# The last chunk's transposes after layer 0's projection: a new order of left-over pieces at the start of the attention

## The chip, the cores and the metric

The kernel runs on one core of one Trainium2 chip. The metric is the device time of one execution in microseconds (us), as the median of several runs. The engines are TensorE (PE in the profile; PEld is its weight load), VectorE (DVE), ScalarE (ACT), GpSimd (POOL) and SyncE (SP), which issues most of the DMAs.

## The reference

Two layers work on an image `x` of 2 x 128 x 64 x 64 in float32. Layer 0 is a neighbourhood attention with an MLP behind it; layer 1 is a full attention over 4096 tokens per image, and then a spectral convolution. What matters here, cut:

```python
# layer 0, for each image, on x transposed to tokens
y = _ln(x, g1, be1)
y = _na2d(y, qkv_w, qkv_b, rpb, proj_w, proj_b)   # 7 x 7 neighbourhood, 4 heads, then proj
y = _ln(y, g2, be2) @ w1.T + bl1
x = y + r
y = relu(_ln(x, g3, be3) @ w2.T + bl2)
x = _ln(y, g4, be4) @ w3.T + bl3 + x
# layer 1
t = _to_tokens(x)
q = _ln_t(t)
sim = einsum('blh,bmh->blm', q, q) * scale          # diagonal masked
t = t + einsum('blm,bmh->blh', softmax(sim), q)
t = t + _L1_ffn_ref(_ln_t(t), ...)                   # spectral filters, as a convolution
```

## The kernel before, in words

**Layer 0** is cut into 16 bands, eight for each image, of 8 rows x 64 columns = 512 tokens. The work on one band is cut into some 70 small pieces, each a closure kept by name: `p.` for the projections to q, k and v, `u0` to `u3` for the four attention units, `r.` for the division by the softmax's sum, `t.`, `t1.`, `t2.`, `t3.` for the output projection and the MLP with its norms. A table, `PLAN`, gives each piece a time; a band is started each `PERIOD`. All pieces of all bands are sorted by these times into one list of events, which is executed with a manual schedule: the order written is the order on PE, DVE, ACT and POOL.

**Pieces of the next layer among them.** While image 1 goes through layer 0, image 0 is prepared for the attention of layer 1, in eight chunks of four token tiles, one chunk for each band of image 1. These pieces begin with `k.`: `k.a` (transposes of `xa`, L196), `k.tt` (copy by ScalarE, L683), `k.bn` (statistics by VectorE, L690 and L692), `k.pw` (the power -1/2 by POOL, L697 and L698), `k.z` (four normalised tiles `tok` by POOL, L703), `k.b` (four transposes of `tok` by TensorE, recorded at L189 with inputs `ident,tok`) and `k.cm` (the copy to `cm` by ScalarE, L715).

**What is left over.** Pieces of the last bands that would come after the last attention unit of layer 0 aren't executed there. They are put into the list `later` (65 pieces of the bands 12 to 15: the ends of the MLP and the norms); the seven `k.` pieces of the last band are put into `chunk_`. The list executed later is `chunk_` followed by `later`. The first pieces of `later` are `t.proj` of band 15 (the output projection, four products at L601, which read `att`), `t.pb` of band 15 (VectorE adds the bias, L612), `t.yr` of band 12 (POOL, L659), `t.add` of band 12 (POOL, L635 and L637) and `t3.bn` of band 12 (VectorE, L378 and L380). Behind them stand, among others, `t3.pw` (POOL, L385 and L386), `t3.nb` (VectorE, L395), `t3.zd` (VectorE, L415), `t3.za` (ScalarE, L406), the same five of `t1` for band 15, `t3.tr` (transposes of `z`, L189), `t3.zT` (copy by ScalarE, L428) and `t.w3` (the product at L332).

**The attention of layer 1** takes pairs of chunks (a, c), a <= c. For a pair, `weights` makes four products of 128 x 512 (L898), of which ScalarE makes the exponentials `e` with their sums (L905); where a = c VectorE adds the diagonal first (L903). For a = c the products with `tok` go onto `own` (L926). For a < c they go onto `other` (L951), and the exponentials are also turned: `turned` transposes four 128 x 128 blocks into a bank (L912), and VectorE copies them out as `et` and adds up their sums (L915); the products of `et` go onto `own` (L926). The products of the next pair are issued ahead of those of this one.

**What is filled in.** After each product the attention calls `fill`, which takes one step of the first generator that has one. The first is `drain`: it executes the left-over list, three pieces to a step. Here the order isn't manual: the framework's scheduler orders the instructions of the attention and of the pieces, by its own plan, on each engine. In it the last chunk's `k.b` of before stands on TensorE behind three of the first four products onto `own`, and ahead of the third product of the pair (0, 1) and of `t.proj`. The banks that the pieces and the attention use come from one ring of six.

**Other work at this place.** `branch_weights` (VectorE, L1068 to L1109; POOL raises `sg` to a power at L1065) and `filters` (VectorE copies `pn` to `ph`, L1142, from DMAs that SP issues at L1136) run through the same stretch. Behind the attention of image 0 comes that of image 1, and then the convolution (products at L1306, copies at L1307, products with the filter matrices at L1318).

Of the kernel before, what the change touches and what calls it, by code (L numbers as in the profile page):

```python
# [93 lines left out]
def kernel(  # L94
# [125 lines left out]
    with l0a:  # L220
# [611 lines left out]
        now, later, chunk_ = [], [], []  # L832
        for at, k, name, f in events:
# [4 lines left out]
            else:  # L838
                early = True
            (chunk_ if name[:1] == "k" and k == bands[-1] else now if early else later).append(f)  # L840
        later = [*chunk_, *later]
        engines = mybir.EngineType
        with tc.manual_schedule(engines={engines.PE, engines.DVE, engines.Activation, engines.Pool}):
            for f in now:
# [649 lines left out]
```

## Time and profile before

| what | value |
|---|---|
| runs | 2232.13, 2233.68, 2233.82 us; median 2233.68 |
| the profiled execution | 2235.26 us, of which the span from the first to the last instruction is 2233.6 us |
| mean granted TensorE clock over the span | 0.991 |
| layer 1's attention, first product of image 0 (L898) | starts at 352.6 us |
| layer 1's attention, last product of image 1 (L898) | starts at 1284.4 us |
| one product of 128 x 512 (L898, L926, L951) at full clock | 0.86 us in the chain |

The profile is of one execution. Its times count from the span's start. TensorE's float32 products of 128 x 512 stand in it as two records each; a transpose of 128 x 128 is one record. A matmul's own duration holds the time until its last result, so following ones overlap it; the chain of waits gives the pace. "Idle before" and the name behind the arrow say how long an engine stood ahead of an instruction, and what was finished last before it went on. The granted clock is the share of full speed that TensorE had in a stretch.

### The profile page before, as it was taken

The numbers are of one execution on the slowest core, as the hardware profiler recorded it, in microseconds if no ns is written. First come the engines' busy times: TensorE is split into PE (matmuls) and PEld (weight loads), VectorE is DVE, ScalarE is ACT, GpSimd is POOL, SyncE is SP. The second block draws the span as 40 slices with busy tenths as digits, with TensorE's granted clock in tenths as the row PEclk, the third lists the DMA queues.
The fourth block names the chain that finished last, engine by engine and source line by source line (L and its number), as shares of the span: only waits on it lengthen the run. The fifth ranks groups of instructions, "written<-read, shape, count | busy, mean of one in ns | idle before, by whom it ended". The sixth has DMA issues, their size and how long they took to land.

```text
span 2233.6 us, 31536 instructions
## 1 busy us (share of the span) xinstructions
PE 2165.4 (97%) x11856; PEld 1333.8 (60%) x11856; DVE 932.9 (42%) x3038; ACT 783.4 (35%) x1904; POOL 276.7 (12%) x353
## 2 busy tenths in 40 slices
PE   5899998999999999999999999999999999999998
PEld 3577774544454444544544447677677777777766
DVE  4799985434443346433333342222213232323232
ACT  2789983222332223222222332322323232222232
POOL 3367874200000000000000000000000000000000
PEclk8999998999999999999999999999999999999999
DMA  4222222011000016100000122222222121212101
GB/s 110 72 62 61 61 55 51 1 57 62 24 24 22 8 44 181 38 24 15 10 24 24 47 82 68 50 48 59 47 51 59 39 59 39 59 39 59 40 10 76
DMA packets 174810, 109.53 MB, mean 49 GB/s; under 512 B 26049, under 2 KB 159809, under 8 KB 174146
## 3 DMA queue, kind: packets, MB, share of 16 engines
q1 hardware_dynamic: 171818, 105.24, 18.0%
q10 hardware_dynamic: 2840, 2.27, 0.4%
q8 instruction: 94, 1.54, 0.3%
q14 instruction: 58, 0.48, 0.1%
HBM read 72.87 MB, written 34.60 MB: 48 GB/s over the span
## 4 chain that ended last, share of the span: by engine, by line
PE 86%; DVE 6%; POOL 3%; DMA 2%; ACT 1%; issue 1%; SPq 1%; ACTq 0%; POOLq 0%; DVEq 0%
PE acc L1318 25%; PE pc L1306 13%; PE bank L898 10%; PE own L926 10%; PE other L951 8%; PE bank L912 4%; PE bank L332 2%; PE bank L189 2%; PE bank L542 2%; PE bank L1011 1%; PE bank L1043 1%; PE py L1340 1%; DMA st<-in_m_minus_dram 1%; PE po L564 1%; PE bank L506 1%
## 5 line engine op out<-in xcount | busy, mean ns | idle before, releaser
L1307 DVE COPY y<-pc 128x512 f32<-128x512 f32 x320 | 221.6, 692 | 351.5 <-PE pc L1306 347.8
L905 ACT ACTIVATE e<-bank 128x512 f32<-128x512 f32 x288 | 171.9, 597 | 552.5 <-PE bank L898 417.3
L898 PE MATMUL bank<-cm 128*128 128x512 f32 x576 | 298.9, 603 | 1.4 <-DVE y L653 1.4
L1318 PE MATMUL acc<-y,mpl 128*128 128x256 f32 x1280 | 292.1, 382 | 0.0
L1318 PE MATMUL acc<-y,mmi 128*128 128x256 f32 x1280 | 288.0, 379 | 0.0
L1306 PE MATMUL pc<-ct,ut 64*128 64x512 f32 x1280 | 285.2, 595 | 0.9 <-issue 0.9
L1318 PEld LDWEIGHTS acc<-y,mpl 128*128 128x128 f32 x1280 | 238.1, 190 | 59.4 <-issue 29.6
L1318 PEld LDWEIGHTS acc<-y,mmi 128*128 128x128 f32 x1280 | 242.6, 190 | 32.7
L1307 ACT COPY y<-pc 128x512 f32<-128x512 f32 x320 | 205.0, 641 | 86.5 <-PE pc L1306 86.5
L951 PE MATMUL other<-e,tok 128*128 128x512 f32 x448 | 228.6, 592 | 0.0
L926 PE MATMUL own<-et,tok 128*128 128x512 f32 x448 | 227.1, 594 | 1.4 <-DVE part L915 1.4
L915 DVE CUSTOM_DVE_ANT_0 et<-bank,one 128x512 f32<-128x512 f32 x224 | 145.7, 688 | 166.5 <-PE bank L912 166.3
L1306 PEld LDWEIGHTS pc<-ct,ut 64*128 64x128 f32 x1280 | 121.5, 187 | 145.8 <-issue 140.6
L1325 ACT COPY ob<-acc 128x256 f32<-128x256 f32 x32 | 19.3, 604 | 387.0 <-PE acc L1318 387.0
L926 PEld LDWEIGHTS own<-et,tok 128*128 128x128 f32 x448 | 84.4, 190 | 109.7 <-issue 72.6
L951 PEld LDWEIGHTS other<-e,tok 128*128 128x128 f32 x448 | 85.0, 190 | 106.6 <-issue 105.9
L898 PEld LDWEIGHTS bank<-cm 128*128 128x128 f32 x576 | 95.7, 193 | 73.8 <-issue 44.7
L1342 DVE TENSOR_TENSOR xa<-py,xa 128x512 f32<-128x512 f32 x32 | 22.1, 692 | 281.4 <-PE py L1340 281.4
L912 PEld LDWEIGHTS bank<-ident,e 128*128 128x128 f32 x896 | 103.3, 142 | 57.2 <-issue 43.6
L161 POOL TENSOR_TENSOR ln_rs<-ln_rs,mhalf 128x4 f32<-128x4 f32 x24 | 24.3, 1012 | 847.6 <-DVE ln_rs L160 847.6
L529 ACT ACTIVATE p<-p,mn 128x196 f32<-128x196 f32 x256 | 114.4, 449 | 22.2 <-DVE mn L519 14.0
L912 PE MATMUL bank<-ident,e 128*128 128x128 f32 x896 | 117.6, 274 | 0.0
(208 smaller groups left out, 2292.4 us busy)
## 6 DMA issues: line engine op xcount, KB each, us to landing
ut<-us SPq DMA_DIRECT2D x80, 256.0 KB
us<-ub SPq DMA_DIRECT2D x64, 256.0 KB
vw<-vd SPq DMA_DIRECT2D x256, 49.0 KB
ct<-gs SPq DMA_DIRECT2D x160, 72.0 KB
ct<-gs SPq DMA_DIRECT2D x160, 64.0 KB
gs<-sum SPq DMA_DIRECT2D x20, 256.0 KB
vd<-v SPq DMA_DIRECT2D x128, 32.0 KB
st<-in_m_plus_dram SPq DMA_DIRECT2D x16, 256.0 KB
```

The lines of the kernel that those rows point to most:

```text
L189: nc.tensor.transpose(ps[:, j * P : (j + 1) * P], src[:, j, :], ident)
L332: nc.tensor.matmul(pl, lhsT=wg[:, lo : lo + P], rhs=zT, start=True, stop=True)
L529: nc.scalar.activation(p, p, AF.Exp, bias=t[name + "mn"][:, h : h + 1], scale=-1.0, accum_out=t["den"][:, u, h : h + 1],)
L898: nc.tensor.matmul(ps, lhsT=cm[b][:, n * P : (n + 1) * P], rhs=cm[b][:, chunk(c)], start=True, stop=True)
L905: nc.scalar.activation(e, ps, AF.Exp, bias=0.0, scale=ASCALE, accum_out=part[:, n, c : c + 1])
L912: nc.tensor.transpose(pt[:, k * P : (k + 1) * P], es[k][:, m * P : (m + 1) * P], ident)
L915: nc.vector.tensor_tensor_reduce(et, pt, one, 1.0, 0.0, ALU.mult, ALU.add, part[:, n, a : a + 1])
L926: nc.tensor.matmul(own, lhsT=tok[b][:, n, :], rhs=e, start=first, stop=last)
L951: nc.tensor.matmul(other, lhsT=tok[b][:, 4 * CHUNKS[a] + j, :], rhs=es[j], start=(j == 0), stop=(j == 3))
L1306: nc.tensor.matmul(pc, lhsT=ut[fp, b, par, :], rhs=cv_[fp], start=True, stop=True)
L1307: (nc.scalar.copy if f else nc.vector.tensor_copy)(y[:, 4 * f : 4 * f + 4, :, par, b * 2 * FB + q : (b + 1) * 2 * FB : 2], pc.rearrange("p ...
L1318: nc.tensor.matmul(acc, lhsT=(mmi if l else mpl)[:, k, :], rhs=y[:, 1::2, k, ::-1, :] if l else y[:, 0::2, k, :, :], start=(l == 0 and k = ...
```

## The change

The list of left-over pieces is no longer `chunk_` and then `later`. In the diff, `chunk_[:3]` is `k.a`, `k.tt`, `k.bn`; `later[2]` is `t.yr` of band 12; `chunk_[3:5]` is `k.pw`, `k.z`; `later[:2]` is `t.proj`, `t.pb` of band 15; `later[3:5]` is `t.add`, `t3.bn` of band 12; `chunk_[5:]` is `k.b`, `k.cm`. So `t.yr` comes ahead of `k.pw`, and the four other pieces of `later` come ahead of the chunk's transposes. From the thirteenth piece on the list is the same.

```diff
@@ -838,7 +838,8 @@
             else:
                 early = True
             (chunk_ if name[:1] == "k" and k == bands[-1] else now if early else later).append(f)
-        later = [*chunk_, *later]
+
+        later = [*chunk_[:3], later[2], *chunk_[3:5], *later[:2], *later[3:5], *chunk_[5:], *later[5:]]
         engines = mybir.EngineType
         with tc.manual_schedule(engines={engines.PE, engines.DVE, engines.Activation, engines.Pool}):
             for f in now:
```

The pieces are the same ones and compute the same. On the built program's instruction lists, those of POOL, VectorE and SP have the order of before. On TensorE the order after the second product onto `own` is now: third product of the pair (0, 1), third product onto `own`, the four of `t.proj`, fourth product of the pair, fourth onto `own`, the four transposes of `k.b`. Before it was: third product onto `own`, the four transposes of `k.b`, third product of the pair, the four of `t.proj`, fourth product of the pair, fourth onto `own`. On ScalarE, `k.cm` now stands behind the exponentials of the third and fourth product of the pair and behind `t3.za`, and both halves of `t1.za` stand ahead of the exponentials of the pair (0, 2). Four of these allocations (`k.b`, `t.proj`, third and fourth product of the pair) get another bank of the ring.

## The prediction

> **What bounds the kernel now.** I read the page's shares first, then the chain of waits, then the timelines of the engines around the change. From the page:
>
> ```profile
> PE 2165.4 (97%) x11856; PEld 1333.8 (60%) x11856; DVE 932.9 (42%) x3038; ACT 783.4 (35%) x1904; POOL 276.7 (12%) x353
> ...
> PE 86%; DVE 6%; POOL 3%; DMA 2%; ACT 1%; issue 1%; SPq 1%; ACTq 0%; POOLq 0%; DVEq 0%
> ```
>
> TensorE is the bound nearly everywhere, so a time lost on it is a time lost at the end, unless another queue then becomes late. A part of POOL's 3% of the chain lies just where the attention begins. The chain there (start, us, what):
>
> ```profile
> 356.32 1.76 POOL y L659
> 358.09 3.29 POOL sg L1065
> ...
> 362.82 3.37 POOL tok L703 x4
> ...
> 366.24 0.48 PE bank L189
> 366.71 1.71 PE bank L898 x2
> 368.42 1.71 PE bank L601 x8
> 370.13 1.69 PE bank L898 x2
> 371.81 0.86 PE own L926 x2
> ```
>
> POOL ends last until 366.2: its queue is unbroken, and its last four instructions (k.z) make the tokens that the last chunk's transposes (k.b, L189) read. Then TensorE takes over, and each job of it costs 1.7 us where the same job costs 0.86 us from 371.8 on. TensorE's timeline says what it did meanwhile (the brackets are the idle time ahead):
>
> ```profile
> 359.10 1.88 PE L926 MATMUL own<-e,tok 128*128 128x512 f32 x4
> 363.68 0.33 PE L189 MATMUL bank<-ident,tok 128*128 128x128 f32 x1 [2.70 <-POOL tok L703]
> 364.68 0.37 PE L189 MATMUL bank<-ident,tok 128*128 128x128 f32 x1 [0.68 <-POOL tok L703]
> 365.46 0.47 PE L189 MATMUL bank<-ident,tok 128*128 128x128 f32 x1 [0.41 <-POOL tok L703]
> 366.24 0.48 PE L189 MATMUL bank<-ident,tok 128*128 128x128 f32 x1 [0.30 <-POOL tok L703]
> ```
>
> TensorE stands for 2.70 + 0.68 + 0.41 + 0.30 = 4.09 us, with ready products queued behind the waiting transposes. The busy times by stretch (columns: PE, PEld, DVE, ACT, POOL, granted clock, DMA) show the second half of the price:
>
> ```profile
> 361.00:362.00 1.00, 0.00 (x0) 0.00 (x0) 1.00 (x9) 0.00 (x0) 0.92 (x3) 1.00 1.31 113
> 364.00:365.00 1.00, 0.32 (x2) 0.14 (x1) 0.48 (x2) 0.00 (x0) 1.00 (x2) 0.92 1.28 69
> 371.00:372.00 1.00, 1.00 (x2) 0.33 (x2) 1.00 (x8) 0.15 (x1) 0.00 (x0) 0.67 0.05 15
> ```
>
> Between the last two rows the clock is 0.50. A mean of 0.92 puts the fall at 364.84, one of 0.67 the return at 371.66. The idle stretch thus costs twice: the wait, and a slow start after it.
>
> [...]371.66 - 364.84 = 6.82 us, two windows. [...]VectorE's L1142 pair runs at 368.14, behind an L395 that waited 3.06 us for POOL.
>
> **The change part by part.** Steps moved: t.yr and t.add of band 12 (1 and 3 POOL instructions), t3.bn of band 12 (8 on VectorE), t.proj and t.pb of band 15 (4 products; 1 on VectorE), k.pw and k.z (2 and 4 on POOL), k.b (4 transposes) and k.cm (1 on ScalarE). None issues a DMA. In the built program the orders on POOL, VectorE and SP are those of before (the scheduler had them there already); only TensorE and ScalarE change. So POOL still ends k.z at 366.2, and those three orders cost nothing.
>
> TensorE: four jobs now stand ahead of the transposes: an L898, t.proj's L601 (eight records), an L898 and an L926, each 0.86 us at full clock: 3.44 us. The PE queue would end them at 360.85 + 3.44 = 364.3. The transposes then go as tokens come, the last at 366.24, and the next L898 starts at about 366.36. The four jobs' inputs are all early: att was written at 348.7, the exponentials that free their banks ended by 358.6.
>
> Without a new wait the first L926 on a turned tile (378.54 in before) is reached after L898, L951, L898, L951, L912 x8, L898, L951: 7 x 0.86 = 6.0, at 372.4. In before the same road from 366.36 has eleven jobs: 11 x 0.86 = 9.5, which gives 375.85 at full clock; the trace has 378.54, so 2.7 us went to half clock (5.42 us of work between 366.24 and 371.66, half of it lost: 2.71).
>
> The clock in after: the idle time left is about 1.5 us, scattered over 364.3 to 366.2. A window holding all of it is still 56% busy. Windows of before that I could lay on the grid: 14% busy lost the clock, 60 to 80% mostly kept it (the one from 334.11, 60% and made of small products, lost it). I take full clock; the other end is one or two half-clock windows, 1.7 to 3.4 us of TensorE time.
>
> New wait, VectorE: the turned tile needs L915, which stands behind the statistics of band 15. VectorE in before:
>
> ```profile
> 368.14 0.67 DVE L1142 COPY ph<-pn 128x256 f32<-128x256 f32 x2
> 370.17 0.69 DVE L612 TENSOR_TENSOR x<-bank,add 128x512 f32<-128x512 f32 x1 [1.36 <-PE bank L601]
> ...
> 373.52 0.16 DVE L395 SCALAR_TENSOR_TENSOR ln_nb<-ln_mv,ln_rs 128x4 f32<-128x4 f32 x1 [1.48 <-POOL ln_rs L386]
> 373.60 0.60 DVE L415 TENSOR_SCALAR z<-x,ln_mv,ln_rs 128x128 f32<-128x128 f32 x2
> ```
>
> L612 no longer waits for L601 and follows L1142 at 368.75, 1.42 us sooner. Its chain keeps its lengths: statistics, POOL's power, L395 3.35 us after L612, both L415 done at +3.96, so L915 can start at 372.7 and its tile is there at 372.7 + 0.70 = 373.4; with the semaphore 373.5. TensorE, there at 372.4, waits **1.1 us**. Behind that L926 stand four transposes of z and all later products. So the start moves from 378.54 to 373.5: **5.0 us** in this execution. L915 of before started at 376.58 only because TensorE was late; the cover is now gone, and each us that VectorE is later costs one.
>
> ScalarE: both halves of t1.za (L406) now stand ahead of the exponentials of the next pair. L395 then ends at 372.26, so L406 takes 372.3 to 373.2 and the first such exponential 373.1 to 373.7; the product that wants its bank (the L898 after L926 and the transposes) comes at 374.8. The exponential that L912's fourth transpose reads stays behind t3.za, which POOL's power holds until 367.7: it runs 368.5 to 369.2; TensorE asks at 369.8. Covered by 0.6 us. L912's second tile now uses t.proj's bank, freed by L612 at 369.4, wanted at 370.2. All cost nothing; each turns into a wait if its margin goes. k.cm ends at about 369.8 and only the transposes of z, at 374.4, ask for its bank.
>
> After that the order is that of before, and TensorE ends last again, so 5.0 us should reach the end: 2235.26 (the profiled execution, 2233.6 of span and 1.7 around it) becomes 2230.2.
>
> Against the median of the runs: the grid lies differently in each. [...]work at half clock after 366.24 lasts 3.4 to 6.8 us and costs 1.7 to 3.4[...]. I take 2.4, an estimate, not this execution's 2.7. Then 375.85 + 2.4 - 373.5 = 4.7 us, and 2233.68 - 4.7 = **2229.0**. The 373.5 hangs on POOL and VectorE and does not vary with the grid; the spread is 3.5 to 5.9 us, 2227.8 to 2230.2.
>
> **The rivals.** *The clock falls all the same*, as the remaining 1.5 us may fall into one window[...]. For: the 60% window from 334.11. Against: windows from 351.18 and 852.94, about as empty, kept it. 1.7 to 3.4 us of loss, of which the 1.1 us of waiting at L926 hide part: the gain shrinks to 2.4 to 4.1, 2229.6 to 2231.3.
>
> *The wait moves on*: VectorE or ScalarE is one to three us later than worked out (L395's chain, or the 0.6 us margin at L912), TensorE stands for 2 to 4 us at L926: 2229.9 to 2231.9. For: three margins below 1 us. Against: each length is read from rows of these very instructions.
>
> *No second wait*: L926 at 372.4, a gain of 4.7 + 1.1 = 5.8 us, or 6.8 if the longest half-clock stretch is typical: 2226.9 to 2227.9.
>
> *Slower*: VectorE's second L1142 pair waits for a transfer of phi; it stands ahead of L612 and so of L915. In before it was hidden by up to 5 us, now by nothing: one us per us beyond 368.1. Its gain is gone when it lands 4.7 us late, and it is over 0.2% slower from 9.2 us late, 10 us giving 2239.0. Against: the first pair's transfer ended its wait at 363.67, and the second was issued 1.4 us after it.
>
> That the change does nothing is excluded by the instruction order.
>
> **Chances.** As worked out 0.70, clock falls 0.11, wait moves on 0.10, no second wait 0.06, slower 0.03. 0.2%, about what a measurement of this kernel can tell from no change, is 4.5 us: below 2229.2 is faster. The likeliest case straddles that line, with a little more than half below (0.40 of 0.70), and no second wait lies wholly below it; the early ends of the two next cases add little, and the runs' own 1.7 us spread blurs it: faster 0.50, same 0.46, slower 0.04. The range, 2226.8 to 2232.3, takes in the rivals but the slower one, with 0.6 to 1 us for the spread of runs.
>
> **What would show it.** Right: L189 on tok begins near 364.3 with under 1 us of listed idle in all; L898 behind it 0.86 us, not 1.7; no clock of 0.5 between 364 and 372; L612 at about 368.8 without waiting; TensorE idle about 1 us ahead of the first L926 on et, released by VectorE L915, at about 373.5; the attention's end some 5 us sooner. Wrong: half clock after 366, an idle above 2 us at L926 or L912, a wait of L898 for ScalarE's e near 375, or later waits that take the gain back.

## The result, and the profile after

| what | before | after |
|---|---|---|
| median of 13 runs each, taken together | 2235.32 us (2232.13 to 2237.53) | 2231.14 us (2227.11 to 2233.32) |
| ratio, with its 95% interval | | 0.9979 [0.9970, 0.9987] |
| the profiled execution | 2235.26 us | 2231.67 us |
| its span | 2233.6 us | 2229.9 us |
| the attention's first product of image 0 | 352.57 us | 352.94 us |
| POOL ends `k.z` | 366.18 us | 366.19 us |
| first product of a turned tile onto `own` | 378.54 us | 373.42 us |

The ratio says 4.7 us faster (0.0021 x 2235), between 2.9 and 6.7; the single times of one kernel spread by more than that. The diff adds an empty line, so lines behind it count one more: L899 is L898 of before, L913 L912, L916 L915, L927 L926, L952 L951, L1066 L1065, L1143 L1142. The page's shares moved little:

```profile
PE 2162.2 (97%) x11856; PEld 1332.3 (60%) x11856; DVE 932.4 (42%) x3038; ACT 781.9 (35%) x1904; POOL 276.3 (12%) x353
...
PE 85%; DVE 6%; POOL 4%; DMA 2%; ACT 1%; SPq 1%; issue 1%; ACTq 0%; POOLq 0%; DVEq 0%
```

TensorE lost 3.2 us of busy time, with the same 11856 instructions; some 2.7 of them are the products that ran at half clock at this place in before. The chain of waits around the change (start, us, what):

```profile
362.80 3.39 POOL tok L703 x4
366.19 0.21 POOL ln_rs L385
...
368.82 0.61 DVE x L612
...
371.01 1.05 POOL ln_rs L386
...
372.76 0.60 DVE et L916
...
373.42 1.13 PE own L927 x2
```

In before the chain went from POOL's `tok` into TensorE's transposes. Now it never touches TensorE between 362.80 and 373.42: it stays with POOL, goes through VectorE's bias and statistics and POOL's second power, and comes to TensorE with `et`. TensorE's timeline shows both stretches, with the idle time in brackets:

```profile
363.79 1.02 PE L927 MATMUL own<-e,tok 128*128 128x512 f32 x2
364.65 0.38 PE L189 MATMUL bank<-ident,tok 128*128 128x128 f32 x2
365.47 0.33 PE L189 MATMUL bank<-ident,tok 128*128 128x128 f32 x1 [0.44 <-POOL tok L703]
366.25 0.33 PE L189 MATMUL bank<-ident,tok 128*128 128x128 f32 x1 [0.45 <-POOL tok L703]
366.41 1.02 PE L899 MATMUL bank<-cm 128*128 128x512 f32 x2
...
373.42 1.13 PE L927 MATMUL own<-et,tok 128*128 128x512 f32 x2 [0.82 <-DVE part L916]
```

Two transposes find their tile ready; two wait 0.89 us together, where four waited 4.09 us before. The product behind them is 0.86 us ahead of the next, not 1.7. And there is a wait that before did not have: 0.82 us for `et`. (From start to start it is 373.42 - 371.58 = 1.84 us for a job of 0.86, so 0.98 lost.) The busy times by stretch (PE, PEld, DVE, ACT, POOL, granted clock, DMA share, GB/s) have full clock at the place where before had half:

```profile
364.00:365.00 1.00, 1.00 (x4) 0.28 (x2) 0.70 (x2) 0.00 (x0) 1.00 (x2) 1.00 1.66 106
365.00:366.00 1.00, 0.36 (x2) 0.14 (x1) 0.00 (x0) 0.00 (x0) 1.00 (x2) 1.00 0.35 27
371.00:372.00 1.00, 1.00 (x3) 0.38 (x2) 0.00 (x0) 0.00 (x0) 0.99 (x1) 1.00 0.06 16
```

VectorE's timeline shows why `et` comes when it does:

```profile
368.73 0.69 DVE L612 TENSOR_TENSOR x<-bank,add 128x512 f32<-128x512 f32 x1
...
372.08 0.16 DVE L395 SCALAR_TENSOR_TENSOR ln_nb<-ln_mv,ln_rs 128x4 f32<-128x4 f32 x1 [1.48 <-POOL ln_rs L386]
372.16 0.60 DVE L415 TENSOR_SCALAR z<-x,ln_mv,ln_rs 128x128 f32<-128x128 f32 x2
372.67 0.68 DVE L916 CUSTOM_DVE_ANT_0 et<-bank,one 128x512 f32<-128x512 f32 x1
```

L612 no longer waits for L601. The tile's copy stands behind L395, which waits 1.48 us for POOL. It starts at 372.67 and takes 0.69 us, while TensorE has ended the job before (371.58 + 0.86 = 372.44) and has nothing else ahead of this product.

**The gain at the place.** From the end of `k.z` to the first product of a turned tile it was 12.35 us and is 7.23. It adds up: four jobs of 0.86 us are gone from this road (3.44), the half clock is gone (2.7: half of the 5.42 us between the last transpose at 366.24 and the clock's return at 371.66; what 12.35 leaves over 0.2 for the last transpose and 11 jobs x 0.86 is 2.7 too), and the new wait is added (0.98). 3.44 + 2.7 - 0.98 = 5.16, against 5.12 seen. Against a second profile of before (run e9 below, 11.13 us) the gain is 3.9, since the half clock took less there. The two mean 4.5, which fits the 4.7 of the timing.

The end of `k.z` is at 366.18 and 366.19 us by a coincidence: the attention began 0.37 us later in after, and POOL's power for `sg` took 2.93 us there against 3.31.

**Why the two profiles differ by less at the end.** The spans differ by 3.6 us. What lies between is the same to 0.1 us but for two stretches in which the clock fell in one of the two executions: at 859.8 us in before, of which 0.2 us is left over by 920 us, and at 1292.2 us, where the attention gives way to the convolution, in after. The latter in the busy times of after:

```profile
1292.00:1296.00 4.00, 4.00 (x12) 1.47 (x12) 0.87 (x2) 1.67 (x2) 0.00 (x0) 0.57 0.07 18
```

The clock is 0.57 there, and it is 1.00 in before. In both traces every half-clock stretch lasts 3.41, 6.83 or 20.48 us, that is one, two or six times 3.41, but for the last one, which the end of the trace cuts; "window" below means such a piece of 3.41 us. From the attention's last product onto `own` to the first product of the convolution it is 37.65 us in after and 35.95 in before. Such a fall begins between 1289 and 1296 us in three of the six profiles with the transposes early (e2, e3, e5) and in three of the six with the transposes late (after, e1, e8), so these 1.7 us at the end belong to the execution and not to the change: 5.1 + 0.2 - 1.7 = 3.6.

### The profile page after: what moved, and what is told of

Same layout as the page of the kernel before. It is cut to its first block, busy times and chain, and to the rows that moved or that the text cites. A ratio compares the mean times of both kernels' runs of the same rounds, so it can differ in the third digit from the quotient of the medians.

```text
span 2229.9 us, 31535 instructions
## 1 busy us (share of the span) xinstructions
PE 2162.2 (97%) x11856; PEld 1332.3 (60%) x11856; DVE 932.4 (42%) x3038; ACT 781.9 (35%) x1904; POOL 276.3 (12%) x353
## 4 chain that ended last, share of the span: by engine, by line
PE 85%; DVE 6%; POOL 4%; DMA 2%; ACT 1%; SPq 1%; issue 1%; ACTq 0%; POOLq 0%; DVEq 0%
PE acc L1319 25%; PE pc L1307 13%; PE own L927 10%; PE bank L899 9%; PE other L952 8%; PE bank L913 4%; PE bank L332 2%; PE bank L189 2%; PE bank L1044 2%; PE bank L542 1%; PE bank L1012 1%; PE py L1341 1%; DMA st<-in_m_minus_dram 1%; PE po L564 1%; PE bank L506 1%
## 5 line engine op out<-in xcount | busy, mean ns | idle before, releaser
L899 PE MATMUL bank<-cm 128*128 128x512 f32 x576 | 296.8, 599 | 1.4 <-DVE y L653 1.4
L927 PE MATMUL own<-et,tok 128*128 128x512 f32 x448 | 227.3, 594 | 3.4 <-DVE part L916 3.4
L952 PE MATMUL other<-e,tok 128*128 128x512 f32 x448 | 228.6, 592 | 0.0
L916 DVE CUSTOM_DVE_ANT_0 et<-bank,one 128x512 f32<-128x512 f32 x224 | 145.6, 688 | 164.6 <-PE bank L913 164.5
L927 PEld LDWEIGHTS own<-et,tok 128*128 128x128 f32 x448 | 84.2, 190 | 112.4 <-issue 71.1
L952 PEld LDWEIGHTS other<-e,tok 128*128 128x128 f32 x448 | 85.0, 190 | 106.6 <-issue 106.2
L899 PEld LDWEIGHTS bank<-cm 128*128 128x128 f32 x576 | 95.2, 192 | 73.8 <-issue 44.4
L913 PEld LDWEIGHTS bank<-ident,e 128*128 128x128 f32 x896 | 102.9, 141 | 56.5 <-issue 41.9
L913 PE MATMUL bank<-ident,e 128*128 128x128 f32 x896 | 117.2, 274 | 0.0
```

Of the source, the lines that this page charges most:

```text
L899: nc.tensor.matmul(ps, lhsT=cm[b][:, n * P : (n + 1) * P], rhs=cm[b][:, chunk(c)], start=True, stop=True)
L913: nc.tensor.transpose(pt[:, k * P : (k + 1) * P], es[k][:, m * P : (m + 1) * P], ident)
L916: nc.vector.tensor_tensor_reduce(et, pt, one, 1.0, 0.0, ALU.mult, ALU.add, part[:, n, a : a + 1])
L927: nc.tensor.matmul(own, lhsT=tok[b][:, n, :], rhs=e, start=first, stop=last)
L952: nc.tensor.matmul(other, lhsT=tok[b][:, 4 * CHUNKS[a] + j, :], rhs=es[j], start=(j == 0), stop=(j == 3))
```

## The experiments

The theory: three sizes make the gain, namely four jobs in the place of TensorE's idle time, a clock that no longer falls, less a new wait for VectorE. Rivals: the clock is no cost of its own; the cause is another order of POOL's and VectorE's pieces, or ScalarE's; the gain is POOL's, whose work ends last on the chain. ScalarE's new order and the other banks have no run of their own. But in before TensorE lists no wait for ScalarE or for a bank between 359 and 379 us, so there was none that they could have removed.

**1. The transposes later, alone.** The list without the other moves: `t.yr` stays behind `k.z`.

```diff
-        later = [*chunk_, *later]
+        later = [*chunk_[:5], *later[:4], later[4], *chunk_[5:], *later[5:]]
```

> The transposes of the last chunk stand behind t.proj and behind the two products around it, as in the changed kernel, but t.yr of band 12 keeps its place behind k.z in the list. The scheduler then also puts L612 ahead of the first L395 on VectorE. Theory (the gain is the four TensorE jobs that now fill POOL's stretch, and the clock that stays up): from the end of k.z on POOL to the first product of own on a turned tile about 7 us as in the changed kernel (7.2), not 12.4 as in before; idle time ahead of the transposes about 1 us; no half clock behind them; because L612 is early, the wait ahead of that product shrinks from 0.8 to about 0.5 us. Rival (moving t.yr ahead of k.pw is what helped): 10 us or more. One time, about 2231 us in the first case, near 2235 in the second.

Measured: 2232.97 us in one run, a time that occurs with both kernels and so decides nothing. From the end of `k.z` to the turned tile's product it is 6.85 us, the transposes wait 0.25 + 0.45 us, and the clock does not fall there. TensorE and VectorE at this place:

```profile
373.27 1.12 PE L926 MATMUL own<-et,tok 128*128 128x512 f32 x2 [0.44 <-DVE part L915]
```

```profile
362.68 0.66 DVE L612 TENSOR_TENSOR x<-bank,add 128x512 f32<-128x512 f32 x1
```

So the place of the transposes makes the gain at this spot, and the order of `t.yr` makes none of it. The order is not quite that of the change in this build: `t.proj` stands two products earlier on TensorE, and VectorE has L612 six microseconds sooner than after the change (362.68 against 368.73). TensorE's wait for `et` is 0.44 us, not 0.82, which is the 0.4 us by which this road is shorter than after the change.

**2. Kept busy while it waits.** Before's order, with five products ahead of the last chunk's transposes; the transposes overwrite their results. They take the idle time. The scheduler also moves one product onto `own` behind the transposes.

```diff
+            if b == NB - 1 and g == NG - 1:
+                for _ in range(5):
+                    nc.tensor.matmul(t["kb"], lhsT=cm[0][:, 0:P], rhs=cm[0][:, 0:512], start=True, stop=True)
```

> The order of before, with five additional products of 128 x 512 into the transposes' own bank ahead of them; the transposes overwrite them, so nothing is left out. TensorE still waits for POOL's last token tile, but is kept busy for 4.3 us of the wait. The scheduler moves one product of own behind the transposes (0.86 us). Theory (the wait cost twice, once as idle time and once as half clock): no half clock behind the transposes, and from the end of k.z to the first product on a turned tile 0.2 + 12 x 0.86 = 10.5 us instead of 12.4 in before's profile; time about 1.5 us below before (2.4 of half clock less 0.9 for the moved product). Rival (the half clock is no cost of its own, the idle time is all): 12.4 + 0.9 = 13.3 us, and 0.9 us above before. Second rival[...]: half clock from about 365 as in before.

Measured: median 2235.87 us of 13 runs, beside 2234.98 of 19 for before; ratio 0.9998 [0.9990, 1.0006]. The trace answers more plainly. TensorE's timeline of this kernel, whose products behind the transposes have the number L901:

```profile
359.73 4.46 PE L713 MATMUL bank<-cm 128*128 128x512 f32 x10
...
365.66 0.33 PE L189 MATMUL bank<-ident,tok 128*128 128x128 f32 x1 [0.45 <-POOL tok L703]
365.83 1.02 PE L901 MATMUL bank<-cm 128*128 128x512 f32 x2
```

The granted clock is 1.00 in each stretch from 362 to 374 us. From `k.z` to the turned tile's product it is 10.58 us; the rival without a clock cost expected 13.3. Twelve jobs at full clock and 0.2 are 10.5. At the place the half clock is thus a cost, and work of no use removes it. This kernel has one job more on the road than before (0.86 us), so that of the half clock some 1.4 us should be left over as a gain in the whole time. Over the whole time this timing does not show it.

**3. The same kernel again**, in another set of runs beside before.

> The warm wait once more (the order of before, five additional products ahead of the transposes, overwritten by them), since its first timing could not tell 1.5 us from nothing. Theory (the half clock cost 1.4 to 2.8 us in before, the moved product costs 0.9): 10.5 us from the end of k.z to the first product on a turned tile, and 0.5 to 1.9 us below before in time, 1.3 as the middle. Rival (the half clock costs nothing): equal to before or 0.9 us above it.

Measured: median 2233.91 us of 13 runs, ratio 0.9991 [0.9982, 0.9999], 2.0 us faster, between 0.2 and 4.0. At the place it is 10.57 us, again without half clock. By their ratios the two timings are 0.4 and 2.0 us faster. That agrees with the 1.4 from the profiles, but the first can't be told from no gain and the second only just: the cost of the half clock is shown at the place, not in the whole time.

**4. POOL's longest item out of the chain, in before.** POOL's power for `sg` (3.29 us in before's chain) and the load of its tile go to where the filter matrices are made, later.

```diff
-        sg = tp.tile([P, KF], F32, name="sg")
...
-            nc.sync.dma_start(out=sg, in_=sigma.partition_broadcast(P))
...
-            quarter = sp.tile([P, KF], F32, tag="quarter", name="quarter")
-            nc.gpsimd.memset(quarter, 0.25)
-            nc.gpsimd.tensor_tensor(sg, sg, quarter, ALU.pow)
...
+            nc.sync.dma_start(out=sg, in_=sigma.partition_broadcast(P))
+            quarter = sp.tile([P, KF], F32, tag="quarter", name="quarter")
+            nc.gpsimd.memset(quarter, 0.25)
+            nc.gpsimd.tensor_tensor(sg, sg, quarter, ALU.pow)
...
+        sg = l1.tile([P, KF], F32, name="sg")
```

> The order of before, with POOL's power of sigma (L1065 in before, 3.3 us in the chain just ahead of k.pw) moved into the next attention, with its load. Rival reading of the chain (POOL's queue is the bound, so 3.3 us less on it bring k.z forward by 3.3 us): k.z ends 3 us sooner relative to the attention's first product, the transposes' wait falls from 4.1 to about 1 us, and the half clock is gone; about 2230 us. Theory (k.pw also needs the statistics of VectorE, which ended at 361.04, only 0.3 us ahead of the power's end): k.z comes 0.3 us sooner, the wait stays near 3.8 us, the half clock stays, and the time is that of before within its spread of 2232 to 2237.5.

Measured: 2234.75 us in one run. From the attention's first product to the end of `k.z` it is 13.17 us, against 13.61 in before: 0.44 sooner, for 3.29 us of work taken away. Against the second profile of before (e9), where the power took 2.92 us and the stretch 13.33, it is only 0.16. POOL's timeline says where the rest went:

```profile
359.80 0.23 POOL L697 TENSOR_SCALAR krs<-kmv 128x4 f32<-128x4 f32 x1 [2.89 <-DVE kmv L692]
```

POOL now stands for 2.89 us until VectorE's statistics are there. In before they were there at 361.04 us, only 0.32 us ahead of the time at which the power let POOL go on (361.36). So the chain named the right releaser, and yet removing it was worth no more than the distance to the next one. The transposes wait 3.68 us, the clock falls for 6.83 us, and it is 12.52 us from `k.z` to the turned tile's product: before's price, once more.

**5. and 6. VectorE 2.1 us later, in before and in after.** Three copies of t.pb's bank ahead of L612, overwritten by it, in the last band.

```diff
+            for _ in range(3 if b == NB - 1 and g == NG - 1 else 0):
+                nc.vector.tensor_copy(t["x1"], t["pp"])
```

> The order of before, with three additional copies of t.proj's bank on VectorE ahead of L612 (into the tile that L612 overwrites; nothing is left out), about 0.61 us each, 1.8 us together. Theory (in before VectorE's chain to the turned tile was covered, because TensorE came so late): the turned tile is there 1.8 us later, of which TensorE sees at most 0.6 us: from the end of k.z to the first product on a turned tile 12.4 to 13.0 us. Rival (VectorE's chain costs the same in both orders): 14.2 us.

> The changed kernel with the same three additional copies on VectorE. Theory (the cover is gone, TensorE waits for VectorE's chain to the turned tile): the product on the turned tile comes the full 1.8 us later, 9.0 us behind the end of k.z instead of 7.2, and the wait ahead of it grows from 0.8 to about 2.6 us. Rival (the 0.8 us there is TensorE's own or the semaphore's, not VectorE's queue): 7.2 to 7.6 us.

Measured in before: 2232.41 us in one run. TensorE does not wait for `et`, and from `k.z` to the turned tile's product it is 11.38 us:

```profile
375.52 1.02 PE L928 MATMUL own<-et,tok 128*128 128x512 f32 x2
```

The clock fell for one window of 3.41 us here, not two, so that the 12.4 to 13.0 of the expectation did not apply; the profile of before's order with the same single window (run e9) has 11.13 us. The difference of 0.25 us is the window's place: in this run all 3.41 us of it lie behind the start of the last transpose, of which half is 1.7, in e9 2.94 us do (365.19 to 368.13), of which half is 1.5. Of VectorE's 2.1 us nothing is left over.

Measured in after: 2233.36 us in one run, 9.40 us from `k.z` to the product, 2.17 more than after's 7.23. TensorE's line of that product, and the busy times behind it:

```profile
375.89 1.59 PE L928 MATMUL own<-et,tok 128*128 128x512 f32 x2 [2.99 <-DVE part L917]
```

```profile
374.00:376.00 2.00, 0.11 (x1) 0.12 (x2) 1.46 (x6) 1.26 (x4) 0.51 (x1) 1.00 0.00 0
376.00:378.00 2.00, 2.00 (x6) 1.14 (x7) 0.44 (x2) 0.77 (x3) 0.00 (x0) 0.60 0.00 0
378.00:380.00 2.00, 2.00 (x5) 0.97 (x4) 0.00 (x0) 0.59 (x1) 0.00 (x0) 0.54 0.00 0
```

So VectorE's queue ahead of `et` costs nothing in before and all of its time in after: the cover is gone. Not expected was what the wait of 2.99 us brought with it: from 376.4 us the clock is half for 3.41 us, and from this product to a later one onto `own` it is 236.57 us where it is 234.87 in after, another 1.7 us. The wait of one microsecond in after had no slow clock behind it in either of its profiles.

**7. before and 8. after once more.** Run e9 is before unchanged, e10 is after unchanged.

> The kernel before once more, for a second look at where the half-clock stretches lie. Theory (the wait of 4.1 us always lets the clock fall, and only the windows' place varies from run to run): a half-clock stretch of 3.4 or 6.8 us begins between 362 and 367 us again, and from the end of k.z to the first product on a turned tile it takes 11.4 to 13 us; falls at about 859 and 1292 us may or may not be there. Rival (the fall in the first profile was chance): no half clock there, 9.7 us.

> The changed kernel once more. Theory (the remaining 1 us of idle time at the transposes doesn't reach the clock): no half-clock stretch begins between 362 and 372 us in this profile either; from the end of k.z to the first product on a turned tile 7.2 us; 4 to 5 us below before. Rival (the clock falls there in some runs, by the windows' place): a stretch of 3.4 us from about 366, with the product on the turned tile still near 7.2 to 8.5 us, and runs that spread into two groups.

Measured for before: 2232.04 us in one run; the transposes wait 2.33 + 0.45 + 0.77 + 0.45 = 4.00 us, and it is 11.13 us from `k.z` to the product. The busy times:

```profile
367.00:368.00 1.00, 1.00 (x5) 0.84 (x4) 0.74 (x3) 1.00 (x4) 0.00 (x0) 0.50 0.00 0
368.00:369.00 1.00, 1.00 (x8) 0.76 (x7) 0.28 (x1) 0.14 (x2) 0.00 (x0) 0.94 0.08 22
```

Here the clock is back at 368.12, after one window, where the first profile had two. Measured for after: median 2231.44 us of 21 runs, before 2235.67 of 33, ratio 0.9982 [0.9976, 0.9989]; 7.21 us from `k.z` to the product, no half clock between 362 and 372. Every one of the four profiles with before's order of the transposes and no work put in their way (before, e3, e5, e9) had the fall there; none of the six with the transposes later (after, e1, e6, e7, e8, e10) had it before 374 us.

**9. Two of the four tokens by VectorE, in after.** POOL's four tiles share out, so that the transposes needn't wait at all.

```diff
-                nc.gpsimd.tensor_scalar(
+                eng = nc.vector if b == NB - 1 and g == NG - 1 and j < 2 else nc.gpsimd
+                eng.tensor_scalar(
```

> The changed kernel, with two of the last chunk's four token tiles made by VectorE instead of POOL. Theory (what remains of the stall is POOL's k.z ahead of the transposes, and POOL's power behind it that holds VectorE's queue): tokens ready 1.7 us sooner, no idle time at the transposes; POOL's power behind k.z ends about 1.6 us sooner, L612 at about 1.5 us sooner, the product on the turned tile about 1.5 us sooner than in the changed kernel, with a wait of about 0.8 us ahead of it; time 1.5 us below the changed kernel, some 5.5 to 6 us below before. Rival (the second load of phi, landing about 366.3, or the two tiles' own time on VectorE, holds L612): the wait ahead of the product on the turned tile grows to 2 us or more and the time is that of the changed kernel.

Measured: median 2228.67 us of 7 runs, ratio 0.9968 [0.9956, 0.9979]. The four transposes run without idle time, the wait for `et` is 0.84 us, and from the attention's first product to the turned tile's it is 19.19 us against 20.48 in after. Both roads became 1.3 us shorter: TensorE's, by what was left of the wait at the transposes, and that to `et`, on which POOL's first power starts 1.3 us sooner behind its two tokens. The wait between them stayed.

**10. The same, with the list of run 1.** VectorE's bias comes early there, which should take the wait for `et` too.

> The order of the run with the transposes late alone (t.yr unmoved, so that VectorE has L612 ahead of its first L395), and two of the last chunk's four token tiles made by VectorE. Theory (two limits are left: the tokens, and VectorE's queue ahead of the turned tile; this shortens both): tokens 1.3 us sooner than in the changed kernel, no idle time at the transposes, and the wait ahead of the product on the turned tile at or below 0.5 us; from the attention's first product to that on the turned tile 19.0 us or less (20.5 in the changed kernel, 19.2 with shared tokens alone); time at or a little below that with shared tokens (2228.7). Rival (POOL's power for the second norm or the second load of phi sets the turned tile whatever L612's place): 19.2 us and the same time.

Measured: median 2228.41 us of 7 runs, ratio 0.9971 [0.9960, 0.9982]; 18.59 us, and the wait for `et` is down to 0.26 us:

```profile
370.72 1.12 PE L927 MATMUL own<-et,tok 128*128 128x512 f32 x2 [0.26 <-DVE part L916]
```

Both versions are faster than before. That they are faster than after by 1.3 and 1.9 us is seen at the place; in the whole time the intervals of the three overlap.

## Why the prediction was right

**POOL sets the end of `k.z`, and the four jobs fill its stretch.** Right: `k.z` ended at 366.19, predicted 366.2; the transposes began at 364.65, predicted 364.3 (the attention began 0.37 later); the product behind them began at 366.41, predicted 366.36. That `k.z` agrees to 0.01 us is luck: the attention's later start and the shorter power cancelled. Run 1 shows that this step makes the gain without the move of `t.yr`; run 4 shows that shortening POOL's chain by its largest item would not have, for VectorE's statistics stood behind it.

**The clock does not fall.** Right: the granted clock is 1.00 from 359 to 379 us in after. That it would stay was the author's estimate from a few windows of before. Run 2 shows that the half clock is a cost of its own at the place: 10.58 us from `k.z` to the turned tile's product, where the rival without a clock cost expected 13.3. The rival in which it falls all the same did not come.

The edges of the half-clock stretches lie whole windows apart within a trace: in before, 81 windows from the return at 61.05 us to the fall at 337.53, and 143 from the return at 371.66 to the fall at 859.77; in after, 82 from 59.95 to 339.84, and 277 from 346.67 to 1292.16. This is the grid of which the prediction speaks; laid on these edges, the windows show how busy TensorE was ahead of the fall. In before:

```profile
361.42:364.83 3.41, 0.48 (x2) 0.28 (x2) 1.47 (x8) 0.00 (x0) 3.21 (x5) 1.00 1.47 89
```

That is 14%; in e3, e9 and e5 it was 19, 28 and 34%. With the transposes later, or with run 2's products, no window that began between 357 and 372 us was less than 73% busy (74% in after; the prediction's 56% was too careful), and the clock stayed. No sharp limit shows. In before a window of 45% from 856.35 us lost the clock and one of 53% from 1293.26 kept it; in after one of 53% from 1288.75 lost it and one of 44% from 848.43 kept it. In layer 0 one of 61% from 334.11 us lost it in before, where after kept it with 61% from 333.02 and lost it with 73% from 336.43.

**The half clock is worth 2.4 us on average.** Right as far as can be told; where between 1.7 and 3.4 us the mean lies was the author's estimate. Above the road at full clock (0.2 + 11 x 0.86 = 9.66 us), the four profiles of before's order (before, e3, e9, e5) have 2.7, 2.9, 1.5 and 1.7 us: 2.2 in the mean, and two sizes rather than one. Each is half of the slow time behind the start of the last transpose (5.42, 5.77, 2.94 and 3.41 us). Two windows followed where the first slow one was 79 and 83% busy (before, e3), one where it was 87 and 100% busy (e9, e5). That is no rule: in before the slow window from 40.57 us was 100% busy, and five more followed it. Four profiles are few for a mean. The spread's upper end of 5.9 us does not come out of the prediction's own terms: 375.85 + 3.4 - 373.5 is 5.75. Nothing rests on it.

**The wait moves to L915, 1.1 us.** Right: 0.98 us, behind L395 and POOL's power, with `et` used at 373.42 (predicted 373.5). Runs 5 and 6 show that the cover is gone: 2.1 us more on VectorE made no difference before that the window's place does not explain, and 2.17 us now. ScalarE's margins held; TensorE lists no wait on it there.

**5.0 us in the profile.** 5.12 us at the place, but 3.6 in the profiled time (2231.67, predicted 2230.2). The step "TensorE ends last again, so 5.0 us should reach the end" is right about the work in between and left out the clock: a half-clock window at 1292 us in this execution took 1.7 us that the execution of before did not pay there.

**4.7 us against the median: 2229.0.** The ratio gives 4.7 us too. So close an agreement is luck: its interval runs from 2.9 to 6.7, and the ratio of the second timing (run 8) gives 4.0. That the time is 2231.14, 2.1 us above the prediction, has its larger part in the starting point: the median of before was 2233.68 of three runs and is 2235.32 of thirteen, 1.6 us more. The medians of the two sets of thirteen are 4.2 us apart, which leaves 0.5. The range held. No rival came.

What stays open: why some falls far from the change (at 834 to 860 and at 1292 us) come in one execution and not in the next. Counted back from the edges in whole windows, the first one begins 3.02 us behind the span's start in before and 1.92 us in after; why it lies there no run shows, and none moved it on purpose.

## What to carry to other kernels

Put ready work ahead of an instruction that waits for a slower engine: in before TensorE stood for 4.09 us with ready products behind the waiting transposes, in after for 0.89. Where the engine that waits is TensorE, a wait of three or four microseconds had a second price in all five profiles that have one at this place, the slow clock behind it: 1.5 to 2.9 us. Before you count the gain, look at what stands ahead of the next tile in the next engine's queue: work that was hidden behind the old wait becomes the new one (0.82 us for `et` in after). When you take an item out of a chain of waits, look for the releaser next behind it: its distance is all that you can win. And compare two traces by local distances, here from one engine's event to another's, for half-clock windows elsewhere change a whole run by as much as such an edit does: the second profiles of the two kernels (2232.04 and 2231.08 us) differ by 1.0 us in the whole and by 3.9 at the place.

## What was not expected of the hardware

A wait of 2.99 us on TensorE amid full work (run 6) was enough for a half-clock window of 3.41 us, at a cost of 1.7 us; two microseconds with four transposes and 0.89 us of listed idle time (after) were not. In run 6 the wait lay, but for 0.1 us, in one window (373.01 to 376.42 us), in which TensorE was busy for 0.53 us. Where two windows share such a wait, both came: TensorE's wait for the L178 that makes `z` lies 1.3 us in one and 1.9 us in the next in before (3.21 us, to 858.22), and the clock fell at 859.77; in after it lies 1.9 and 1.2 us (3.14 us, to 853.07), and the clock stayed. The same program with the same wait of 4.0 to 4.1 us paid one slow window in one execution and two in another (e9, and the first profile), 1.2 us apart at the place. And one kernel's runs spread over 6 us (after: 2227.11 to 2233.32), where each half-clock window that comes or goes is some 1.7 us.
